# Folding two layer norms into weights, statistics of two tiles at once and one bank for four heads' sums, in a two-layer graph-attention, Mamba and LSTM kernel

## The chip, the cores and the metric

The kernel runs on one core of a Trainium2 chip. The metric is the time of one launch in microseconds of the device. Times given are medians of several runs; the profile is that of one further execution. The engines are named as the profile names them: PE (TensorE, matrix multiplication; its weight loads are PEld), DVE (VectorE), ACT (ScalarE), POOL (GpSimd) and SP (SyncE, which here only starts DMAs).

## The reference, cut to what matters

There are 32 batches of 512 rows of 256 features, and an integer adjacency of 512 x 512 for each batch. Four residual blocks follow each other, each on the normalised features (`_layernorm`: mean out, divided by the root of variance plus 1e-5):

```python
x = x + L0_gnn(_layernorm(x), adj, ...)   # 4 heads of 64; softmax over neighbours; relu + h; a norm per head; gamma, beta
x = x + L0_ffn(_layernorm(x), ...)        # Mamba-2 block: projection, convolution of 4 taps, decayed products, gate, norm, projection
x = x + L1_gnn(_layernorm(x), adj, ...)   # one head of 256; softmax over neighbours; elu
x = x + L1_ffn(_layernorm(x), ...)        # LSTM over 512 steps, with prefix and suffix sums
```

The first three blocks treat every batch by itself ("the layers" below). The LSTM runs over all 32 batches together, one row after another ("the recurrence"); it needs the layers' result of every batch.

## The kernel before, in words

**The whole.** `tile_adj_ffn_kernel` (L1569) calls `layers_per_batch` (L154), which writes the layers' result to `X3` in DRAM, and then `recurrence` (L1290). Between them stands a branch: if a check on the data failed (`odd`), the layers are done again by a general form (`attention0`, `attention1`). With these inputs that form isn't run.

**Tiles.** A batch's features are a tile of 128 partitions x 4 row tiles (`NT`) x 256 columns. Six generators make up a batch: `plain0` (L587, layer-0 attention), `after0` (L428, the norm per head and the residual), `mamba_in` (L703), `mamba_dt` (L715), `mamba` (L788) and `plain1` (L1042, layer-1 attention).

**The order of the work.** It is written out by hand. A `Recorder` (L89) takes down the operations of one batch as units: each operation off PE is a unit, and a run of PE operations into one PSUM bank is a unit. The table `PLAN` (L1535) gives each unit a due time; batch b's units get `PERIOD * b` more (L1145); all units of all batches are sorted by that (L1147) and issued in that order on each engine's queue, which works in order. So every engine has work of three batches mixed: in the steady state PE turns batch b's features and does its attention sums, does the Mamba part of batch b-1 and the layer-1 attention of batch b-2. Buffers and the eight PSUM banks (`LazyPool`, L70) are given out in the same order. The preparation of the recurrence's weights (`recurrence_weights`, L1180) goes on POOL and its DMA queue, in 49 pieces with due times from 32.6 to 34.6 periods (L1133), so among the last batches' units.

**The parts that the change touches.**
- `layernorm` (L138): four `bn_stats` and four `bn_aggr` on DVE, a variance-to-factor step on POOL (`rstd_of`, L129: one `tensor_scalar`, one power), `off` on DVE, and four ACT operations that write the normalised tile (`xn` in `plain0`, `xm` in `mamba_in`, `xg` in `plain1`). Then `transposed` (L369) turns it on PE, eight transposes into two banks, and ACT copies both out.
- `plain0`: `xT` (the turned `xn`) times `w0` gives `hn` (256 features and 12 score columns), copied out by ACT. After the exponents, DVE makes 16 tiles `w` of 128 x 512 (L582), four for each pair (q, m) of a pair of heads and a pair of column tiles. PE multiplies them into `pav` (64 output partitions for each head, L653) and into `psu` (the sums of the softmax, L661):

```python
h, r = 2 * q + k, 32 * (2 * k + t)
nc.tensor.matmul(
    psu[r : r + 32, :], cols[:, 1, h, j : j + 1].to_broadcast([P, 32]), w[:, t, k, :],
    start=(m == 0), stop=(m == NT // 2 - 1),
)
```

  So the four sums of a unit (two column tiles t, two heads k) go to four different quarters of the 128 output partitions. There is one `psu` bank for each q; each is copied by ACT (`avs`), turned by four transposes (`psut`), and DVE adds the two quarters of a head.
- `after0`: for each half of the tile, DVE adds, takes the mean per head, centres; ACT squares; DVE sums the squares; POOL makes the factor; DVE multiplies; POOL applies gamma and the residual.
- `plain1` and `after1` (L984): `xg` is turned and multiplied by `w1`; scores, exponents, four products `pov`; ACT scales each out (`ov`), POOL takes the minimum with zero (`em`, two operations of 128 x 512), ACT the exponential, DVE adds in two operations of 128 x 1024, and the result goes to `X3`.

An f32 matmul in the source is two PE instructions in the profile, and an f32 transpose is one.

Of the kernel before, what the change touches and what calls it, by code (L numbers as in the profile page):

```python
# [9 lines left out]
F32 = mybir.dt.float32  # L10
# [3 lines left out]
AF = mybir.ActivationFunctionType  # L14
ALU = mybir.AluOpType
# [137 lines left out]

def layers_per_batch(ctx, tc, c, a, X3, odd=None, wr=None):  # L154
# [68 lines left out]
    lane = wp.tile([P, 32], F32, name="lane")  # L223
    nc.vector.tensor_reduce(lane, c.ident.rearrange("p (i k) -> p k i", k=32), AX.X, ALU.add)
# [76 lines left out]
    else:  # L301
# [11 lines left out]
        for k in range(DK):  # L313
            pw = score_weights1(k)
            for to, n, f in ((0, 0, 0.8), (1, 1, -0.8), (2, 1, 1.0)):
                nc.vector.tensor_scalar(w1[:, k, D + to : D + to + 1], pw[:, n : n + 1], f, None, ALU.mult)

# [110 lines left out]
    def after0(b, state):  # L428

        x, o, hn = (state[k] for k in ("x", "o", "hn"))  # L430

        G = NT // 2 * H0
        halves = [slice(n * NT // 2, (n + 1) * NT // 2) for n in range(2)]
        ogs = []
        for n, r in enumerate(halves):
            nc.vector.scalar_tensor_tensor(o[:, r], o[:, r], 0.0, hn[:, r, :D], ALU.max, ALU.add)
            og = o[:, r].rearrange("p i (h e) -> p (i h) e", h=H0)
            mean = small.tile([P, G], F32, tag="mean", name=f"mean{b}_{n}")
            nc.vector.tensor_reduce(mean, og, AX.X, ALU.add)
            nc.vector.scalar_tensor_tensor(  # L440
                og, mean.unsqueeze(2).to_broadcast([P, G, HO]), -1.0 / HO, og, ALU.mult, ALU.add
            )
            ogs.append(og)
            yield
        sq = two.tile([P, NT, D], F32, tag="rowa", name=f"sq{b}")
        for n, r in enumerate(halves):
            nc.scalar.activation(sq[:, r], o[:, r], AF.Square)
            vs = small.tile([P, G], F32, tag="vs", name=f"vs{b}_{n}")
            nc.vector.tensor_reduce(vs, sq[:, r].rearrange("p i (h e) -> p (i h) e", h=H0), AX.X, ALU.add)
            rs = rstd_of(nc, small, c, vs, G, 1e-6, scale=1.0 / HO)  # L450
            nc.vector.tensor_tensor(ogs[n], ogs[n], rs.unsqueeze(2).to_broadcast([P, G, HO]), ALU.mult)
            nc.gpsimd.tensor_tensor(o[:, r], o[:, r], gamma.unsqueeze(1).to_broadcast([P, NT // 2, D]), ALU.mult)
            nc.gpsimd.tensor_tensor(x[:, r], x[:, r], o[:, r], ALU.add)
            yield
# [132 lines left out]
    def plain0(b, state):  # L587
# [8 lines left out]
        xn = two.tile([P, NT, D], F32, tag="rowa", name=f"xn{b}")  # L596
        layernorm(nc, small, c, xn, x, NT)
# [7 lines left out]
        yield  # L605
        xT = transposed(xn, "xT", f"xT{b}", psa)
        yield
        hn = one.tile([P, NT, D + 3 * H0], F32, tag="hn", name=f"hn{b}")
        for it in range(NT):
# [6 lines left out]
            nc.scalar.copy(hn[:, it, :], pp[:, : D + 3 * H0])  # L616
# [24 lines left out]
        sums = sall[:, b, :H0, :]  # L641
        for q in range(2):
            rb = spread(line, 2 * q, 2, f"{b}_{q}")
            pa = bank(f"pav{b}_{q}", psa)
            psu = bank(f"psu{b}_{q}", psa)
            for m in range(NT // 2):
# [10 lines left out]
                for t in range(2):  # L657
                    j = 2 * m + t
                    for k in range(2):
                        h, r = 2 * q + k, 32 * (2 * k + t)  # L660
                        nc.tensor.matmul(  # L661
                            psu[r : r + 32, :], cols[:, 1, h, j : j + 1].to_broadcast([P, 32]), w[:, t, k, :],
                            start=(m == 0), stop=(m == NT // 2 - 1),
                        )
                yield
            nc.scalar.copy(avT[:, q, :], pa)
            avs = two.tile([P, N], F32, tag="avs", bufs=1, name=f"avs{b}_{q}")
            nc.scalar.copy(avs, psu)
            pst = bank(f"psut{b}_{q}", psa)
            for i in range(NT):  # L670
                nc.tensor.transpose(pst[:, i * P : (i + 1) * P], avs[:, i * P : (i + 1) * P], c.ident)
            nc.vector.tensor_reduce(
                sums[:, 2 * q : 2 * q + 2, :],
                pst.rearrange("p (i k t r) -> p k i t r", i=NT, k=2, t=2)[:, :, :, :, 0], AX.X, ALU.add,
            )
            yield
        nc.vector.tensor_scalar(sums, sums, TINY, None, ALU.max)
# [25 lines left out]
    def mamba_in(b, state):  # L703
# [3 lines left out]
        layernorm(nc, small, c, xm, x, NT)  # L707
# [334 lines left out]
    def plain1(b, state):  # L1042

        x, adjT = state["x"], state["adjT"]
        xg = two.tile([P, NT, D], F32, tag="rowa", name=f"xg{b}")
        layernorm(nc, small, c, xg, x, NT)
        yield
        gT = transposed(xg, "xT", f"gT{b}", psa)
        yield
        wb = one.tile([P, NT, D + 1], F32, tag="hb", name=f"wb{b}")  # L1050
        pps = []
        for it in range(NT):
# [6 lines left out]
            nc.vector.tensor_copy(exp1[-1][:, it, :], pp[:, D : D + 3])  # L1059
# [3 lines left out]
        yield  # L1063
        for it in range(NT):
            nc.scalar.activation(wb[:, it, :D], pps[it][:, :D], AF.Copy, scale=cols[:, 1, 0, it : it + 1])
# [7 lines left out]
        v = two.tile([P, NT, D], F32, tag="rowa", name=f"ov{b}")  # L1073
        for it in range(NT):
# [8 lines left out]
            rinv = small.tile([P, 1], F32, tag="rinv1", name=f"rinv1_{b}_{it}")  # L1083
            nc.vector.reciprocal(rinv, sums)
            nc.scalar.activation(v[:, it, :], po[:, :D], AF.Copy, scale=rinv)
            yield
        yield from after1(b, x, v)
# [4 lines left out]
    if odd is None:  # L1092
        first, second = attention0, attention1
        STEPS = {mamba_in: 2, mamba_dt: 4, mamba: 25, after0: 4, first: 40, second: 8}
# [195 lines left out]
def recurrence(ctx, tc, c, a, X3, wr, out):  # L1290
# [245 lines left out]
    20597 0 35607 40650 32723 38571 34106 39730 39719 42522 49516 65141 94900 99741 99103 99067  # L1536
    100351 150138 104650 33299 41504 23661 101407 105289 104391 105410 106002 107466 108253 108405 106965 107971
    106773 107370 108940 111668 111723 112606 112816 113281 114035 114669 116368 116572 115240 61098 62220 95465
    106507 111843 123503 73463 118372 125340 127346 127820 128180 128298 129543 130272 130550 131386 131603 131405
    131637 131643 134967 135471 134528 138394 135989 138827 152511 136294 136633 137827 137029 137053 146560 147251  # L1540
    149455 138638 139934 141008 140407 147466 150878 149492 152286 151960 151986 153816 154238 154424 152813 157240
    157367 161054 165376 165719 161319 162074 165950 173469 180373 183224 175030 175764 178029 178951 183005 185109
    191927 190640 193312 196625 199960 199982 203114 203928 197913 197972 197331 199400 204575 205181 204667 206194
    206643 207386 207758 208322 208515 208599 208862 251501 213317 211809 212124 212008 213030 213570 214990 215312
    216196 217020 218298 218575 218670 219478 220078 220205 220492 222048 222692 222696 222880 223352 223622 224029
    224511 224969 225104 226703 225336 228084 228828 234005 236603 228856 237288 257861 259334 246520 239831 270799
    272731 218148 231463 230092 233713 227439 231438 214083 221469 222635 225691 227899 229011 231018 231069 246057
    256887 246081 256048 282617 251804 253984 257648 218528 231970 232380 237266 238842 239097 237276 242576 246641
    248924 251119 253230 216766 225312 226088 232262 232399 235687 227913 239722 240705 245507 246951 252337 238425
    249887 249750 246294 249203 247281 251894 247953 251981 254197 260686 253343 258102 264985 266809 266922 269026  # L1550
    266471 269157 261075 270793 273399 267554 270245 270803 272881 274277 276867 273113 279346 273455 280926 283101
    281800 282500 249960 258452 266090 258433 267917 257968 267949 263228 259624 268875 272648 272216 284851 285585
    292644 294196 268390 280811 280814 282469 279962 279938 281791 284180 282382 284389 285227 273497 283284 284220
    289134 292788 256753 285591 285805 275446 279221 278218 278209 278399 276825 286716 287237 286683 288183 289091
    295346 297865 290911 294061 295192 295528 297194 309768 297695 301052 299601 300411 304806 306262 308890 309432
    311412 312571 311544 312188 312543 314589 316438 317376 323083 314746 322079 314057 319805 327469 327488 330029
    332590 334303 335468 335528 337464 342615 341500 345713 352910 355616 355950 361013 356131 361074 354475 359605
    361130 362268 362402 362989 363334 363970 364961 366465 366763 367927 373957 373956 370932 376447 374494 367135
    374547 374557 374613 374703 381795 387807 390440 393320 385936 391088 392248 394917 381245 383616 389387 393007
    380288 380823 388220 390423 396431 398648 395810 398642 399666 409034 411932  # L1560
# [95 lines left out]
```

## Time and profile before

| what | us |
|---|---|
| median of three runs (3856.74 to 3864.42) | 3859.15 |
| profiled execution | 3853.91 |
| its span, first to last instruction | 3852.2 |
| layers, from the start to the load of the recurrence's weights | 2541 |
| recurrence and output, from there to the end | 1311 |
| first and last `psu` instruction | 56.5 and 2336.3 |
| PE busy in the whole span | 3417.8 (89%) |
| DVE busy in the whole span | 3256.5 (85%) |
| ACT, POOL busy in the whole span | 2403.0 (62%), 1510.6 (39%) |

The page's chain that ended last begins at 2541 us with the DMA that loads the recurrence's weights, so for the layers it says nothing; they are read from the stretches and the timeline. All recorded units of the layers stand on one line (L102, the Recorder), so groups are told apart by the names of their tiles. A line of a timeline gives the start in us, the length in us, the engine and operation, the tile written `<-` the tiles read, the tile mode or shape, and the number of instructions; the bracket says what the engine waited for.

### The profile page before, as it was taken

To read this page: it belongs to the slowest core of one execution; us is meant where nothing else is said; L and a number is where in the kernel's file an instruction comes from. 1 tells how busy PE (TensorE), PEld (TensorE's weight loads), DVE (VectorE), ACT (ScalarE), POOL (GpSimd) and SP (SyncE) were. 2 spreads that over 40 slices of the span, in tenths; PEclk is the share of its full clock that TensorE was granted. 3 is DMA by queue.
4 is the path that set the end of the run, shared out by engine and by line. 5 is a ranking of instruction groups with operands and counts; after the bars stand their busy time and mean duration, and the time that the engine had idled before them with its cause. 6 is when DMAs were issued, how large, how long until landed. Compare 5 with 4: busy or idle time off the path is not lost. (4 is left out here: it accounts for less than half of the span.)

```text
span 3852.2 us, 117182 instructions
## 1 busy us (share of the span) xinstructions
PE 3417.8 (89%) x47370; PEld 2313.5 (60%) x47370; DVE 3256.5 (85%) x10671; ACT 2403.0 (62%) x6434; POOL 1510.6 (39%) x1581
## 2 busy tenths in 40 slices
PE   5999999999999999999999998668888888888882
PEld 3466566556656656655665664446666666666661
DVE  3888888888888888888888886459999999999997
ACT  2777777777777777777777775435454544444441
POOL 3456556555555655655555566710000000000000
PEclk8999999999999999999999998789999999999996
DMA  3322322222223232232223212221222222222226
GB/s 98 89 91 73 101 85 75 94 86 86 83 93 90 72 102 86 72 95 86 86 83 96 87 61 59 82 66 41 44 46 43 46 43 46 43 46 43 46 40 191
DMA packets 271800, 288.76 MB, mean 75 GB/s; under 512 B 151589, under 2 KB 221953, under 8 KB 269073
## 3 DMA queue, kind: packets, MB, share of 16 engines
q1 hardware_dynamic: 265248, 266.96, 25.0%
q10 hardware_dynamic: 3152, 8.76, 0.7%
q8 instruction: 375, 6.14, 0.7%
q0 software_dynamic: 2848, 5.45, 0.5%
q14 instruction: 177, 1.44, 0.1%
HBM read 227.09 MB, written 37.11 MB: 69 GB/s over the span
## 5 line engine op out<-in xcount | busy, mean ns | idle before, releaser
L1413 PE MATMUL pg<-wall,h 128*32 128x96 f32 x16352 | 559.0, 277 | 176.8 <-DVE h L1495 169.4
L1413 PEld LDWEIGHTS pg<-wall,h 128*32 128x32 f32 x16352 | 374.4, 109 | 350.8 <-DVE h L1495 331.9
L1413 PE MATMUL pg<-wall,xTr 128*32 128x96 f32 (+1 forms) x16384 | 549.0, 274 | 0.0
L1413 PEld LDWEIGHTS pg<-wall,xTr 128*32 128x32 f32 x16384 | 447.2, 110 | 5.2 <-issue 0.3
L132 POOL TENSOR_SCALAR ve<-mv 128x4 f32<-128x4 f32 x32 | 6.3, 195 | 1038.5 <-DVE mv L1337 1038.5
L1472 ACT ACTIVATE z<-pg 128x96 f32<-128x96 f32 x512 | 128.7, 251 | 438.9 <-PE pg L1413 438.9
L102 DVE SCALAR_TENSOR_TENSOR w<-rb,colsa,adjT 128x512 f32<-128x512 f32 x512 | 380.4, 778 | 6.0 <-DMA rb<-linea 6.0
L102 DVE SCALAR_TENSOR_TENSOR acc<-px,convw,acc 128x511 f32<-128x511 f32 (+2 forms) x480 | 335.3, 735 | 7.6 <-ACT acc L102 6.4
L1483 ACT ACTIVATE z<-z 128x32 f32<-128x32 f32 x1024 | 234.7, 229 | 168.5 <-DVE z L1481 100.9
L102 ACT ACTIVATE g<-bc,cs 128x128 f32<-128x128 f32 x1024 | 326.0, 399 | 13.1 <-PE py L102 13.1
L102 PE MATMUL px<-mT,win 128*128 128x512 f32 x640 | 307.2, 603 | 0.0
L102 PE MATMUL po<-wc,xh 128*128 128x256 f32 x1024 | 254.3, 392 | 13.5 <-POOL xh L102 8.4
L102 POOL TENSOR_SCALAR ve<-bnmv 128x4 f32<-128x4 f32 x96 | 18.8, 196 | 626.3 <-DVE bnmv L102 607.7
L102 PE MATMUL pav<-w,hb 128*64 128x512 f32 x1024 | 250.1, 608 | 8.0 <-DVE w L102 8.0
L102 PE MATMUL pov<-wb,wv 128*128 128x257 f32 x1024 | 250.5, 392 | 7.0 <-DVE wv L102 5.8
L1495 DVE STREAM_TRANSPOSE h<-hh 128x32 f32<-128x32 f32 x1024 | 216.4, 211 | 34.8
L102 PE MATMUL pz<-mT,win 128*128 128x512 f32 x512 | 245.4, 602 | 0.0
L102 POOL TENSOR_TENSOR rs<-ve,mhalf 128x4 f32<-128x4 f32 (+1 forms) x192 | 237.8, 1239 | 13.3
L1478 DVE SCALAR_TENSOR_TENSOR ab<-z 128x64 f32<-128x64 f32 x1024 | 226.0, 221 | 15.3 <-ACT z L1472 12.0
L102 PEld LDWEIGHTS po<-wc,xh 128*128 128x128 f32 x1024 | 189.5, 193 | 76.6 <-issue 27.0
L1481 DVE SCALAR_TENSOR_TENSOR z<-ab 128x32 f32<-128x32 f32 x1024 | 196.9, 192 | 35.1
L102 POOL TENSOR_SCALAR msk<-adj 128x1024 bf16<-128x1024 int32 x64 | 218.8, 3434 | 13.0 <-DMA adj<-in_adj_dram 7.9
(258 smaller groups left out, 7987.8 us busy)
## 6 DMA issues: line engine op xcount, KB each, us to landing
bc<-line SPq DMA_DIRECT2D x128, 512.0 KB
adj<-in_adj_dram SPq DMA_DIRECT2D x32, 1024.0 KB
rb<-linea SPq DMA_DIRECT2D x64, 512.0 KB
ce<-line SPq DMA_DIRECT2D x64, 384.0 KB
x<-in_x_dram SPq DMA_DIRECT2D x32, 512.0 KB
X<-x SPq DMA_DIRECT2D x32, 512.0 KB
xt<-X SPq DMA_DIRECT2D x128, 128.0 KB
x<-X SPq DMA_DIRECT2D x128, 128.0 KB
```

The costliest lines, as they stand in the source:

```text
L102: return getattr(getattr(self.nc, engine), op)(*map(real, a), **{n: real(v) for n, v in k.items()})
L132: nc.gpsimd.tensor_scalar(ve, var, scale, eps, ALU.mult, ALU.add)
L1413: nc.tensor.matmul(p[q * GB : (q + 1) * GB, :], lhs[k], w[:, k, q, s:e], start=(start and k == 0), stop=(stop and k == DK - 1),)
L1472: nc.scalar.activation(z[:, H : 4 * H], pgs[0], AF.Tanh)
L1478: nc.vector.scalar_tensor_tensor(ab, z[:, c0 + 2 * H : c0 + 4 * H], 1.0, z[:, c0 : c0 + 2 * H], ALU.add, ALU.mult)
L1481: nc.vector.scalar_tensor_tensor(z2[:, c0 : c0 + H], ab[:, :H], 0.5, ab[:, H:], ALU.mult, ALU.add)
L1483: nc.scalar.activation(z[:, (10 + n) * H : (11 + n) * H], z2[:, 4 * n * H : (4 * n + 1) * H], AF.Tanh, scale=0.5)
L1495: nc.vector.transpose(h[n], half)
```

## The change

- **Raw features are turned.** `plain0` and `plain1` transpose `x` itself. `w0` and `w1` (with their score columns) are centred once at the start: a matmul with ones gives each column's sum, and DVE subtracts 1/256 of it (`centred`). The factor `rs` of each row is applied behind the product: in `plain0` by the ACT operation that copies `hn` out; in `plain1` by the DVE operation that copies the score columns out, and by one factor `rs * cols` in the ACT operation that makes `wb`. `xn`, `xg` and their `off` are gone. `mamba_in` keeps its normalised tile.
- **Statistics of two tiles at once.** `two_stats` gives `bn_stats` two row tiles (or two heads) interleaved element by element, so that its sums of even and odd elements are those of the two tiles; no `bn_aggr` is needed. `after0` uses it in place of the two reductions and ACT's squares.
- **One bank for four heads' sums.** Head h's sums go to the output partitions 32h to 32h+31 of one `psu`, and the two column tiles t of a unit go to the same ones. There is one `avs` copy, four transposes and one DVE operation in place of two, eight and three.
- **ELU.** `plain1` writes relu(v) and relu(-v) from the PSUM bank by two ACT operations for each row tile; one exponential of 128 x 1024 with a factor of -1 follows. POOL's minimum is gone, and each row tile has one more tiny DVE operation (the negated factor).
- **Order.** `PLAN` is made anew: 371 units in place of 395; its latest due time is 440741, it was 411932. `PERIOD` (100234) and the 49 pieces stay. An unused tile `lane` is gone.

```diff
+def two_stats(nc, small, src, n, tag):
+    st = small.tile([P, n // 2, 6], F32, tag=f"st{tag}", name="st")
+    for i in range(n // 2):
+        nc.vector.bn_stats(st[:, i, :], src[:, 2 * i : 2 * i + 2, :].rearrange("p i d -> p d i"))
+    s = st.rearrange("p i (k e) -> p (i k) e", k=2)
+    return s[:, :, 1], s[:, :, 2]
...
+        def centred(w, cols, name):
+            pw = bank(name)
+            for k in range(DK):
+                nc.tensor.matmul(pw[:, :cols], ones, w[:, k, :], start=(k == 0), stop=(k == DK - 1))
+            for k in range(DK):
+                nc.vector.scalar_tensor_tensor(w[:, k, :], pw[:, :cols], -1.0 / D, w[:, k, :], ALU.mult, ALU.add)
@@ after0, for each half r @@
             nc.vector.scalar_tensor_tensor(o[:, r], o[:, r], 0.0, hn[:, r, :D], ALU.max, ALU.add)
+            mean, var = two_stats(nc, small, og, G, "a")
+            nc.vector.tensor_tensor(og, og, mean.unsqueeze(2).to_broadcast([P, G, HO]), ALU.subtract)
+            rs = rstd_of(nc, small, c, var, G, 1e-6, scale=1.0 / HO)
+            nc.vector.tensor_tensor(og, og, rs.unsqueeze(2).to_broadcast([P, G, HO]), ALU.mult)
@@ plain0 @@
-        xn = two.tile([P, NT, D], F32, tag="rowa", name=f"xn{b}")
-        layernorm(nc, small, c, xn, x, NT)
+        xT = transposed(x, "xT", f"xT{b}", psa)
+        _, var = two_stats(nc, small, x, NT, "x")
+        rs = rstd_of(nc, small, c, var, NT, LN_EPS, scale=1.0 / D)
...
-            nc.scalar.copy(hn[:, it, :], pp[:, : D + 3 * H0])
+            nc.scalar.activation(hn[:, it, :], pp[:, : D + 3 * H0], AF.Copy, scale=rs[:, it : it + 1])
...
-                        h, r = 2 * q + k, 32 * (2 * k + t)
+                        h = 2 * q + k
                         nc.tensor.matmul(
-                            psu[r : r + 32, :], cols[:, 1, h, j : j + 1].to_broadcast([P, 32]), w[:, t, k, :],
-                            start=(m == 0), stop=(m == NT // 2 - 1),
+                            psu[32 * h : 32 * (h + 1), :], cols[:, 1, h, j : j + 1].to_broadcast([P, 32]), w[:, t, k, :],
+                            start=(j == 0), stop=(j == NT - 1),
                         )
@@ plain1 @@
-        layernorm(nc, small, c, xg, x, NT)
-        gT = transposed(xg, "xT", f"gT{b}", psa)
+        gT = transposed(x, "xT", f"gT{b}", psa)
+        _, var = two_stats(nc, small, x, NT, "x")
+        rs = rstd_of(nc, small, c, var, NT, LN_EPS, scale=1.0 / D)
...
-            nc.vector.tensor_copy(exp1[-1][:, it, :], pp[:, D : D + 3])
+            nc.vector.tensor_scalar(exp1[-1][:, it, :], pp[:, D : D + 3], rs[:, it : it + 1], None, ALU.mult)
...
+        nc.vector.tensor_tensor(rs, rs, cols[:, 1, 0, :], ALU.mult)
...
+            nc.vector.tensor_scalar(rinv[:, 1:2], rinv[:, 0:1], -1.0, None, ALU.mult)
+            nc.scalar.activation(em[:, it, :], po[:, :D], AF.Relu, scale=rinv[:, 1:2])
+            nc.scalar.activation(v[:, it, :], po[:, :D], AF.Relu, scale=rinv[:, 0:1])
             yield
-        yield from after1(b, x, v)
+        nc.scalar.activation(em, em, AF.Exp, scale=-1.0)
+        nc.vector.tensor_tensor(xf, vf, xf, ALU.add)
+        nc.vector.scalar_tensor_tensor(xf, ef, -1.0, xf, ALU.add, ALU.add)
```

## The prediction, made before the result was known

> **What bounds the kernel now.** I read the page's slices first, then one period of the steady state as a stretch, then PE's timeline in it. The recurrence (from 2541 us) has no line of the change in it, so only the layers can move.
>
> ```profile
> PE   5999999999999999999999998668888888888882
> PEclk8999999999999999999999998789999999999996
> ```
>
> From slice 1 to slice 23 (96 to 2310 us) PE is busy nine tenths or more at the full granted clock. One period there, the stretch from 1155.08 to 1229.15 us (columns: PE, PEld, DVE, ACT, POOL, clock, DMA share, GB/s):
>
> ```profile
> 1155.08:1229.15 74.07, 72.41 (x447) 44.67 (x446) 63.66 (x149) 55.70 (x118) 42.42 (x37) 1.00 0.31 87
> ```
>
> PE works 72.4 of 74.1 us, DVE 63.7, ACT 55.7, POOL 42.4. PE bounds the layers; work taken from the other three counts only where PE waits for it. Busy hides waits, though, because a matmul's recorded length overlaps the next one's start. So I count pitches, from start to start in the timeline: 0.43 us for 512 columns, 0.216 for 256, 0.109 for 128, with two tiles of 64 output columns or four of 32 sharing a pitch. In one batch that makes 62 pitches of 0.43 (px 20, pz 16, pav 16, psu 8, pss 2: 26.6), 96 of about 0.217 (po, pov, pwh, phn: 20.9), 122 of 0.109 (transposes and py: 13.3) and about 4.2 for the small ones: 65.0 us. 22 changes of tile mode at about 0.09 add 2.0. The rest of 74.0, **7.0 us per batch, is waiting in PE's fixed order**. That is all that a lighter DVE, ACT or POOL can give back.
>
> **The one bank (psu): a gain off PE, a price on it.** PE's timeline in that period (tile mode, shape, number of instructions):
>
> ```profile
> 1201.76 1.88 PE L102 MATMUL px<-mT,win 128*128 128x512 f32 x4
> ...
> 1212.61 1.94 PE L102 MATMUL pav<-w,hb 128*64 128x512 f32 x8
> 1214.48 2.69 PE L102 MATMUL psu<-w,colsa 128*32 128x512 f32 x16
> 1217.10 1.94 PE L102 MATMUL pav<-w,hb 128*64 128x512 f32 x8
> ...
> 1221.18 0.60 PE L102 MATMUL psut<-ident,avs 128*128 128x128 f32 x4
> 1221.62 0.60 PE L102 MATMUL pgT<-ident,xg 128*128 128x128 f32 x4
> ...
> 1226.14 1.92 PE L102 MATMUL psu<-w,colsa 128*32 128x512 f32 x16
> ```
>
> Look at pav: eight instructions, two at a time (one for each head's 64 output columns), take 1214.48 - 1212.61 = 1.87 us, four pitches of 0.43 and a change of mode. The second psu run does sixteen in 1.85 us (its successor starts at 1227.99): four pitches, four at a time, because the two heads and the two column tiles lie in four different quarters. After the change the two column tiles of a head share a quarter, so only two run at a time: 8 x 0.43 + 0.13 = 3.57 us for sixteen. Before, the two runs took 2.62 and 1.85 us (the first waited for DVE's w tiles). Sum: 2 x 3.57 - 4.47 = **+2.67 us per batch**. The first run's wait of 0.8 is used up in this. Bounds: could the neighbouring units of the other pair of heads run beside it, nothing would be lost; the instruction order of the changed kernel keeps the pairs apart, so I take the full price.
>
> Four of eight psut transposes go: 1221.62 - 1221.18 = **-0.44 us**. One avs copy (0.57, ACT) and some 0.3 of DVE go beside PE's work: nothing.
>
> **Norms folded.** Gone per batch: eight ACT operations of 0.59 us (xn, xg), two `off` (0.27), and ACT's two squares of 0.63. hn's four copies get a factor (0.38 to about the 0.47 of ov). Statistics: six times two bn_stats (412 ns) and two bn_aggr (171 ns) become six of 512 interleaved elements; two pairs of reductions (0.68 each) in after0 become eight bn_stats of 128. Cost of an interleaved one: at best 0.68 us, as a reduction of 512 elements; at worst 4 x 0.36 = 1.44, by the one small read with a stride in the trace (the tile lane: 360 ns for 128 elements, where 128 in line take 283). I take 0.70, since 412 ns for 256 less the 0.15 of a one-element operation, twice, is 0.52 + 0.15. DVE then sheds 10.6 us and takes on 7.1, so -3.5 per batch (+1.5 at the bad end); ACT sheds about 4.5 in all, POOL 3.0 (em).
>
> The Trainium skill, SBUF — State Buffer, "Door 1: The DMA port swizzle", speaks against this: consecutive accesses within a 16-byte line run at full bandwidth, and each crossing to a new line pays, so f32 may stride freely only within four elements. The interleaved read jumps 1 KB at every element. The lane row leans that way (77 ns more), without a reason shown. By the rule DVE would come out no lighter than before, the waits would stay and the sum would lean to 3924; by the row of bn_stats it is the sum below.
>
> None of this lies on PE. What PE gets is waits, in the new order of instructions: (a) pxT no longer waits for xn: its eight took 1.09 us, 8 x 0.109 = 0.87, so -0.2; (b) po waits for DVE's last xh, 4.04 us for sixteen against 3.46; now eight transposes stand between py and po where four quick pm stood, so -0.4 of 0.6; (c) pm and pqa waited 0.25 for the maximum; now psc and half of po stand between, -0.25; (d) 19 changes of mode in place of 22, -0.27. Together **-1.1 us**. The waits for small DVE chains stay: pqv and pcv still follow each other (about 0.9), pdc and prv too (0.4), and DVE's work ahead of pov sums to the same 9.6 us in both orders. Raw turning brings pgT forward to right behind x's update; its last part comes about when PE gets there: 0, at worst +0.5.
>
> So the period changes by 2.67 - 0.44 - 1.1 = +1.1; for a lighter DVE and ACT I allow -0.1: **+1.0 us x 31 = +31 us**.
>
> **Fill and drain.** At the start pxT of batch 0 waits until 36.1 us for xn, which began at 34.5: -2. The centring (four f32 matmuls, four DVE operations of about 0.5) lies before the last weights arrive, and pwc waits for those until 27.9: 0. At the end nothing covers batch 31:
>
> ```profile
> 2485.43 1.66 DVE L102 SCALAR_TENSOR_TENSOR x<-po,rs,x 128x256 f32<-128x256 f32 x4 [4.56 <-POOL rs L102]
> ...
> 2496.42 1.05 POOL L102 TENSOR_TENSOR rs<-ve,mhalf 128x4 f32<-128x4 f32 x1
> 2497.50 0.16 DVE L102 SCALAR_TENSOR_TENSOR off<-bnmv,rs 128x4 f32<-128x4 f32 x1 [8.82 <-POOL rs L102]
> 2497.76 2.08 ACT L102 ACTIVATE xg<-x,off,rs 128x256 f32<-128x256 f32 x4 [18.81 <-DVE off L102]
> 2498.41 2.80 PE L102 MATMUL pgT<-ident,xg 128*128 128x128 f32 x8 [16.02 <-ACT xg L102]
> ...
> 2503.17 0.16 DVE L102 COPY sc<-pwh 128x3 f32<-128x3 f32 x1 [5.51 <-PE pwh L102]
> ```
>
> x is ready at 2487.1, but the row factor stands on POOL behind pieces of the recurrence's weights until 2497.5, and then xg, pgT and pwh follow. Raw, pgT and pwh run meanwhile; only sc waits for the factor, behind ten rows of pieces in place of thirteen, so about 2495 in place of 2503: -8. ELU without POOL saves 1 more. Pieces lie elsewhere among the last three batches' POOL work now, which may cost or give 10.
>
> **Sum.** +31 - 2 - 9 = +20 on the profiled 3853.9 us, 3874. The median lies 5.2 above that execution: **3879 us**. What 0.2% (8 us) doesn't separate counts as the same, about what a measurement of this kernel can tell.
>
> **Rivals.**
> - *PE's waits close (faster).* Mechanism: the new order with a lighter DVE, ACT and POOL covers the chains in front of PE. It decides once the 7.0 us of waits fall below 4.3: price of psu 3.4 in pitches, less 0.44 and 0.27. At 3.5, period -0.8, so -25 - 11: **3823**. For it: DVE and ACT give up about 4 us each, and every wait named ends at one of the two. Against: the two largest chains stand unchanged in the order.
> - *PE pays all and the order adds waits.* 2.67 - 0.44 = +2.2 x 31 = +68, and little from the drain: **3924**. For it: DVE chain raw to da has 5.2 us of cover where it had 6.9, and interleaved statistics may be slow.
> - *It doesn't show.* Waits fall to just what psu costs: **3859**, within 8 us either way.
>
> **Chances.** Forecast 0.47 (0.05 of it within 8 us of no change), closed waits 0.27, all paid 0.15, nothing to see 0.11. So faster 0.27, same 0.16, slower 0.57. Range 3822 to 3930: the second and third cases at its ends.
>
> **What will show it.** psu sixteen instructions in about 3.6 us each time, pairs 0.43 apart; period 75.0 us between the same tiles of neighbouring batches; PE busy at 97% or more; one bn_stats of 128 x 512 near 0.7 us; pgT of the last batch right behind x. Wrong if four psu still run at once, if the period falls below 74.0, or if DVE's stretch grows above 64 us.

## The result and the profile after

Over six runs each the changed kernel takes 3873.47 us (3871.62 to 3876.31) and the kernel before 3858.14 (3856.67 to 3864.42): a ratio of 1.0039, with a 95% interval of 1.0026 to 1.0052. It is slower by 15 us, 0.4%; the forecast was 3879. The profiled execution takes 3873.03 us, its span is 3871.3 (before: 3852.2).

| us | before | after |
|---|---|---|
| first `psu` of batch 0 | 56.5 | 51.7 |
| from there to the first `psu` of batch 31 | 2267.7 | 2312.5 |
| from there to the load of the recurrence's weights | 217.1 | 197.5 |
| load of the recurrence's weights | 2541.3 | 2561.7 |
| period, mean of batches 3 to 28 | 74.00 | 75.42 |

So the layers lose 45 us in the steady state and win back 5 at the start and 20 at the end; the recurrence is the same within 1.3 us. The page's slices:

```profile
PE   5999999999999999999999998758888888888882
PEclk8999999999999999999999999879999999999996
```

From slice 1 to slice 23 PE is still busy nine tenths or more, at the full granted clock. One period, from one batch's praw to the next (columns as before: PE, PEld, DVE, ACT, POOL, clock, DMA share, GB/s):

```profile
1139.90:1215.32 75.42, 72.65 (x453) 45.11 (x447) 64.11 (x137) 52.17 (x109) 38.45 (x35) 1.00 0.29 85
```

ACT gave up 3.5 us and POOL 4.0, but DVE none: 64.1 where it had 63.7. PE's timeline in that period:

```profile
1141.02 5.32 PE L102 MATMUL px<-mT,win 128*128 128x512 f32 x12
1148.06 0.46 PE L102 MATMUL pcs<-tri,da 128*128 128x128 f32 x2 [1.72 <-DVE da L102]
...
1157.58 1.94 PE L102 MATMUL pav<-w,hb 128*64 128x512 f32 x8
1159.44 3.63 PE L102 MATMUL psu<-w,colsa 128*32 128x512 f32 x16
1163.00 3.65 PE L102 MATMUL pav<-w,hb 128*64 128x512 f32 x16
...
1167.86 3.63 PE L102 MATMUL psu<-w,colsa 128*32 128x512 f32 x16
1171.41 1.94 PE L102 MATMUL pav<-w,hb 128*64 128x512 f32 x8
```

Two things are to be seen. Each psu run takes 3.56 us from its start to its successor's (1163.00 - 1159.44), 7.11 for both, where before it was 4.47. And in front of pcs, the product that makes the running sums of Mamba's decay, PE stands idle for 1.72 us until DVE has written da. The waits of PE over ten batches (600 to 1340 us; columns: total in us, times, longest):

```profile
PE pcs L102 <- DVE da L102: 17.2, 10, 1.7
PE pcv L102 <- DVE args L102: 7.8, 10, 0.8
```

The second line stands in the kernel before with the same numbers; the first has no counterpart there. It comes in every batch, 1.7 us each. The statistics, by form, in the same stretch (columns: busy, mean ns, idle before):

```profile
L102 DVE BATCH_NORM_STATS2 st<-x 128x6 f32<-128x512 f32 x59 | 41.1, 697 | 26.8 <-POOL x L102 26.8
L102 DVE TENSOR_TENSOR o<-o,st 128x512 f32<-128x512 f32 x19 | 21.5, 1134 | 0.0
L102 DVE BATCH_NORM_STATS2 st<-o 128x6 f32<-128x128 f32 x76 | 18.3, 283 | 0.0
```

The interleaved bn_stats takes 697 ns, as forecast. The subtraction of the mean (o<-o,st) takes 1134 on average, where the same shape took 677 before: one of its two takes 1.54 us, the other 0.68. The end of the last batch:

```profile
2516.51 1.66 DVE L102 SCALAR_TENSOR_TENSOR x<-po,rs,x 128x256 f32<-128x256 f32 x4 [4.94 <-POOL rs L102]
...
2517.05 0.72 PE L102 MATMUL pgT<-ident,x 128*128 128x128 f32 x2 [2.24 <-DVE x L102]
...
2524.91 1.05 POOL L102 TENSOR_TENSOR rs<-ve,mhalf 128x4 f32<-128x4 f32 x1
2525.99 0.60 DVE L102 TENSOR_SCALAR sc<-pwh,rs 128x3 f32<-128x3 f32 x4 [6.61 <-POOL rs L102]
```

pgT now starts while x is still being written, and only sc waits for POOL's factor. From the end of x to the start of sc it is 7.8 us (2525.99 - 2518.17); before it was 16.1.

### The profile page after: what moved, and what is told of

It reads as the page before. It is cut to its first block, busy times and chain, and to the rows that moved or that the text cites. A ratio compares the mean times of both kernels' runs of the same rounds, so it can differ in the third digit from the quotient of the medians.

```text
span 3871.3 us, 116194 instructions
## 1 busy us (share of the span) xinstructions
PE 3432.4 (89%) x47250; PEld 2318.6 (60%) x47250; DVE 3268.5 (84%) x10258; ACT 2281.8 (59%) x6178; POOL 1381.7 (36%) x1517
## 5 line engine op out<-in xcount | busy, mean ns | idle before, releaser
L102 DVE SCALAR_TENSOR_TENSOR w<-rb,colsa,adjT 128x512 f32<-128x512 f32 x512 | 354.9, 750 | 37.5 <-PE pav L102 19.6
L102 POOL TENSOR_SCALAR ve<-st 128x4 f32<-128x4 f32 (+1 forms) x160 | 34.8, 218 | 737.9 <-DVE st L102 731.4
L102 PE MATMUL px<-mT,win 128*128 128x512 f32 x640 | 290.5, 592 | 0.0
L102 POOL TENSOR_TENSOR rs<-ve,mhalf 128x4 f32<-128x4 f32 (+1 forms) x192 | 251.5, 1310 | 8.2
L102 PE MATMUL po<-wc,xh 128*128 128x256 f32 x1024 | 246.4, 384 | 8.1 <-POOL xh L102 8.1
L102 PE MATMUL psu<-w,colsa 128*32 128x512 f32 x1024 | 232.1, 595 | 0.0
L102 PEld LDWEIGHTS pov<-wb,wv 128*128 128x128 f32 x1024 | 188.0, 193 | 62.2 <-DVE wv L102 12.1
```

Source lines behind the costliest of these rows:

```text
L102: return getattr(getattr(self.nc, engine), op)(*map(real, a), **{n: real(v) for n, v in k.items()})
```

## The experiments

**What was to be told apart.** Theory: PE bounds the layers; the change costs PE 2.2 us of passes (psu and psut), gives back waits in its order, and adds one wait of 1.7 at pcs. Rivals: DVE sets the period, by its sum or by one full stretch; or the waits swallow the price of psu wherever it is paid. Below, each run is set against runs of the kernel before on the same chip (3851 to 3853 us); by the ratio above the changed kernel stands at 3867 there. A period is the mean of batches 3 to 28. Numbers like 254528 are due times of `PLAN`.

### One bank alone

```diff
 kernel before
-            psu = bank(f"psu{b}_{q}", psa)
+        psu = bank(f"psu{b}", psa)
...
-                        h, r = 2 * q + k, 32 * (2 * k + t)
-                            psu[r : r + 32, :], cols[:, 1, h, j : j + 1].to_broadcast([P, 32]), w[:, t, k, :],
-                            start=(m == 0), stop=(m == NT // 2 - 1),
+                        h = 2 * q + k
+                            psu[32 * h : 32 * (h + 1), :], cols[:, 1, h, j : j + 1].to_broadcast([P, 32]), w[:, t, k, :],
+                            start=(j == 0), stop=(j == NT - 1),
```

One avs, psut and maximum remain, as in the changed kernel.

> The kernel before with the one bank for four heads' sums alone; norms, statistics, ELU and due times as before, only the four units that fall away are taken out of the plan. Theory (PE pays each pass of 512 columns that no longer runs beside another): psu 4.47 to 7.11 us per batch as in the changed kernel, psut -0.44, period 74.03 to about 76.2 us, 31 gaps, so +68: about 3926 us. Rival (PE's waits swallow the price, whatever stands around it): the period grows by the 1.4 us of the changed kernel or less, +43 or less: 3901 or below.

Measured: 3906.45 us, ratio 1.0141 (1.0124 to 1.0158), +54 us; period 75.58, +1.6. psu takes 7.11 us and psut 0.49, exactly the price forecast, but 0.6 of the 2.2 comes back in waits elsewhere (0.3 of it at pdc, 0.2 at pxd). The run lies between the two expectations, 5 us above the rival's bound and 20 below the theory's number: the price is paid in full where psu stands, and over a quarter of it is swallowed by waits elsewhere.

### Everything but the one bank

```diff
 changed kernel: psu, avs, psut and the two reductions for each q as in the kernel before
+  168180 169720 170000    due times of avs, psut and the reduction of q = 0; 179869 for the maximum behind that of q = 1
```

> The changed kernel with the two psu banks of before (four column quarters in use at once, eight psut transposes, two avs copies, DVE's two reductions); four units added to its plan, all other due times unchanged. Theory: psu falls from 7.1 to about 4.0 to 4.5 us, psut rises by 0.44, period 75.4 to about 73.2, 31 gaps: -68, about 3805 us, faster than both kernels. Rival (DVE's w tiles, which come at the same pace, set the end of these runs): psu gains no more than a wait in front of pav and psu gives back; period at or above 74.2, no more than -37: 3836 or above.

Measured: 3805.64 us, ratio 0.9878 (0.9862 to 0.9895), period 73.31. That is the theory's number. PE in this kernel:

```profile
1042.41 0.46 PE L102 MATMUL pcs<-tri,da 128*128 128x128 f32 x2 [1.72 <-DVE da L102]
...
1053.80 2.61 PE L102 MATMUL psu<-w,colsa 128*32 128x512 f32 x16
...
1061.83 1.92 PE L102 MATMUL psu<-w,colsa 128*32 128x512 f32 x16
```

The second psu run is back at four quarters at a time. The first still holds a wait of 0.7 us for DVE's w tiles, and pcs waits as long as in the changed kernel. So the norms, the statistics, ELU and the new order together are worth -47 us, the one bank +54 in the old order; the sum, +7, is 8 us short of the measured +15, so the two don't simply add: in the new order the one bank costs 62 (3867 - 3805.6). How much of the -47 is the order's and how much the operations', no run tells.

### pcs later

```diff
 changed kernel, due times
-  pcs 254528, exp 254970, copy 256673
+  pcs 256560, exp 256600, copy 256673
```

> The changed kernel with one PE instruction group moved: pcs, which waits 1.7 us per batch for DVE's da, stands behind px (tile 1) and pz (tile 2) in place of ahead of them (two due times follow it on ACT). Theory (the wait is a gap in PE's fixed order, with DVE ahead of nothing else there): the wait goes, period -1.7, -53 us: about 3820 us. Rival (the chain of DVE itself sets the pace, and the wait turns up at the next product that needs DVE or ACT): period within 0.4 of 75.4, so 3861 or above.

Measured: 3850.46 us, ratio 0.9990 (0.9980 to 0.9999), period 74.69, -0.7. Neither expectation holds. pcs no longer waits, but:

```profile
1065.83 0.38 PE L102 MATMUL pcs<-tri,da 128*128 128x128 f32 x2
...
1072.08 1.94 PE L102 MATMUL pav<-w,hb 128*64 128x512 f32 x8
1074.92 3.63 PE L102 MATMUL psu<-w,colsa 128*32 128x512 f32 x16 [0.91 <-ACT zs L102]
```

pav takes 2.84 us to psu's start where it needs 1.87: more than half of the wait has moved on by nine microseconds. psu multiplies nothing that zs writes, and zs ends 0.05 us before psu starts; what is left to tie them is a PSUM bank, which zs reads empty. And zs is late because ACT's queue, in order, stood behind DVE:

```profile
1068.03 1.28 ACT L102 ACT_TABLE_LOAD   x1 [1.35 <-DVE acc L102]
...
1072.31 1.99 ACT L102 ACTIVATE sqa<-adj,neghalf 128x2048 bf16<-128x2048 int32 x1
...
1074.29 0.57 ACT L102 ACTIVATE zs<-pz 128x512 f32<-128x512 f32 x1
```

acc stands on DVE's queue behind the chain that ends in da. So what makes da late makes acc late too, and through ACT the bank. Moving PE's step doesn't reach that.

### Both

> The changed kernel with both edits: two psu banks of before and pcs behind px and pz. Theory (PE bound, the two gains add): period about 71.5, -121 us: about 3752. Rival (with PE lighter, DVE's chains in front of pav, pcs or po become the bound, so the gains do not add): no more than 20 us below the better of the two single edits.

Measured: 3805.04 us, ratio 0.9876 (0.9860 to 0.9893), period 73.33: the rival. With two banks nothing at all is left of the gain: px falls by 1.78 us, pav rises by 0.97 (zs again) and psu by 0.73 (0.56 of it a wait for w). DVE never idles for more than 0.5 us from raw to the last w there; whatever makes the start of that stretch late makes its end late.

### Two statistics out of that stretch

```diff
 due times                     with both edits above / with two banks, pcs in its old place
-  bn_stats of x 55396, 354502; ve 370338
+  bn_stats of x 78900, 372700; ve 373500
```

> The changed kernel with the two psu banks and pcs behind px and pz (3805 us), and two of the six 512-element bn_stats moved on DVE from between da and the w tiles to behind the last w (POOL's step after one of them follows). Theory (with pcs out of the way, DVE is the bound in the stretch from raw to the last w, where it never idles for more than 0.5 us): the w tiles come 1.4 us sooner, period 73.3 to about 72.0, -40: about 3765 us. Rival (something else in front of pav and psu sets the pace there, such as the buffers of w or the copies out of px): within 10 us of 3805.

> As the kernel with two psu banks (3805.6 us), pcs in its old place, and the same two bn_stats moved behind the last w. Theory (the wait of pcs for da stands ahead of both and stays at 1.7 us; earlier w tiles then find PE still busy): within 10 us of 3805.6. Rival (the w tiles set the pace even with pcs early): -30 to -40, about 3770.

Measured: 3802.82 us, ratio 0.9864 (0.9848 to 0.9881), period 73.06; and 3815.91, ratio 0.9900 (0.9883 to 0.9916), period 73.58. The first misses its theory and falls in the rival's range. pav does fall back to 7.37 us per batch; but psu still waits 0.55 us for w, and the moved statistics make the factor for sc late, so PE waits 0.54 at prv, where it waited less than 0.2. The second ends 10.3 us above 3805.6, just outside the theory's 10, and not for the theory's reason. The w tiles that come sooner do bring something: psu loses its whole wait of 0.7 us (4.40 to 3.71 per batch), although pcs waits 1.7 as before. But the wait at prv costs 0.6, and pxd, pm and pst behind it another 0.4; so a gain and a loss in one edit hide each other.

### Every statistic twice

```diff
 changed kernel, two_stats
         nc.vector.bn_stats(st[:, i, :], src[:, 2 * i : 2 * i + 2, :].rearrange("p i d -> p d i"))
+        if isinstance(nc, Recorder):
+            nc.units[-1][0].append(nc.units[-1][0][-1])
```

> The changed kernel with every bn_stats of the layers' two-tile statistics issued twice in a row (same input, same output): six of 0.70 us and eight of 0.28 us more on DVE, +6.4 us per batch. Theory (PE's fixed order is the bound and DVE counts only in its full stretch from raw to the last w, in which two of the six stand): +0.6 to +1.4 us per batch, +20 to +45: 3890 to 3915 us. Rival 1 (DVE sets the period with its sum): +6.4 x 31 = +200. Rival 2 (DVE is nowhere on the path): within 8 us of the changed kernel.

Measured: 3981.67 us, ratio 1.0337 (1.0320 to 1.0354), period 78.82, +3.4. All three expectations miss. DVE's added 6.4 us are charged to PE at about one half. They aren't charged by the sum (DVE then works 68.9 of 78.7 us), nor only in the full stretch: PE's waits grow at pcs (2.1), at py for g, at po and in front of psu, which are places where a chain through DVE ends at PE. The half is no pure price, though: the recorded lengths of DVE's instructions grow by 6.1 us, and among them the long o<-o,st falls from 1.54 to 0.68 in this order.

### Pieces earlier

```diff
 kernel before
-    todo = [(PERIOD * (nb + 0.6 + 2.0 / 48 * n), nb, n, [lambda: next(pieces, None)], ()) for n in range(PIECES)]
+    todo = [(PERIOD * (nb + 0.3 + 2.0 / 48 * n), nb, n, [lambda: next(pieces, None)], ()) for n in range(PIECES)]
```

> The kernel before with the 49 pieces of the recurrence's weights due 0.3 periods earlier (32.3 to 34.3), nothing else. Theory (the part of the drain that the forecast missed, 153.0 to 143.7 us from the last batch's psu to its pss, comes from where the pieces fall among the last batches' work on POOL): 5 to 15 us less, between 3838 and 3848 on a kernel before at 3853. Rival (the pieces cost the same wherever they stand, and the 9 us came from the lighter ACT and POOL of the change): within 4 us of before.

Measured: 3848.73 us, ratio 0.9990 (0.9980 to 1.0000), 3 us less: the rival's range. From the last batch's psu to its pss it is 149.7 us where it was 153.0. The place of the pieces is good for 3 of the 9 us at most, by this shift; the last run below, which leaves the pieces alone, has 150.7 there. The rest stays open.

### POOL's msk away from the chain

Why is da late? raw is the step width of the Mamba part, turned by PE; a softplus of it, made of small DVE instructions, gives dt, and dt times aneg is da. msk is the adjacency as a mask of zeros and ones. The chain from raw to da takes 4.85 us in the kernel before, in the changed one 6.69. DVE in the changed kernel, and POOL beside it:

```profile
1065.82 0.19 DVE L102 COPY raw<-praw 128x32 f32<-128x32 f32 x1 [0.30 <-PE praw L102]
1066.04 0.19 DVE L102 SCALAR_TENSOR_TENSOR ee<-raw 128x32 f32<-128x32 f32 x1
1066.53 0.64 DVE L102 TENSOR_SCALAR u<-ee 128x32 f32<-128x32 f32 x1 [0.30 <-ACT ee L102]
...
1067.59 0.19 DVE L102 TENSOR_TENSOR u<-u,ee 128x32 f32<-128x32 f32 x1
1067.82 0.19 DVE L102 TENSOR_TENSOR u<-u 128x32 f32<-128x32 f32 x1
1068.05 0.87 DVE L102 TENSOR_SCALAR q<-u 128x32 f32<-128x32 f32 x1
1068.95 2.11 DVE L102 SCALAR_TENSOR_TENSOR q<-q,u 128x32 f32<-128x32 f32 x6
...
1072.31 0.19 DVE L102 TENSOR_TENSOR da<-dt,aneg 128x32 f32<-128x32 f32 x1
```

```profile
1066.10 5.52 POOL L102 TENSOR_SCALAR msk<-adj 128x1024 bf16<-128x1024 int32 x2
```

The same small instructions took 0.18 (u<-ee, q<-u) and 0.19 each (q<-q,u) in the kernel before, where msk ran 5 us after raw, just behind da:

```profile
1054.47 0.18 DVE L102 TENSOR_SCALAR u<-ee 128x32 f32<-128x32 f32 x1
1055.52 0.18 DVE L102 TENSOR_SCALAR q<-u 128x32 f32<-128x32 f32 x1
```

```profile
1058.60 6.98 POOL L102 TENSOR_SCALAR msk<-adj 128x1024 bf16<-128x1024 int32 x2
```

In the changed kernel u<-ee takes 0.64, q<-u 0.87, and one of the six q<-q,u 0.98: 1.9 us more, while msk runs.

```diff
 changed kernel, due times
-  bn_stats of x 79415, ve 79843, msk 62216 and 69577, pow 379657, x + blin 273531
+  bn_stats of x 72150, ve 72400, msk 72500 and 72600, pow 370900, x + blin 270500
```

msk now stands on POOL behind a step that needs a bn_stats right after the last w.

> The changed kernel (one psu bank, pcs in its old place) with POOL's two msk instructions (2.8 us each) put behind the statistics step that now waits for DVE's bn_stats right after the last w; six due times, no operation added or taken. Theory (while msk runs beside the chain raw to da, three DVE instructions in it take 0.64, 0.87 and 0.98 us in place of 0.18 to 0.19, so the chain takes 6.69 us and not 4.85, and that is the 1.7 us that PE waits at pcs): chain 4.85, wait at pcs near 0, period 75.4 to about 73.7, -53: about 3815 us. Rival 1 (those three are slow for another reason, the chain stays at 6.69): within 10 us of 3868. Rival 2 (the chain shortens but what msk takes from the later POOL work, ce, o and xdd, comes back as a wait): -10 to -30.

Measured: 3814.00 us, ratio 0.9900 (0.9884 to 0.9917), period 73.48: the theory's number, and by its mechanism. The chain of this kernel:

```profile
1041.65 0.19 DVE L102 COPY raw<-praw 128x32 f32<-128x32 f32 x1 [0.30 <-PE praw L102]
...
1042.37 0.18 DVE L102 TENSOR_SCALAR u<-ee 128x32 f32<-128x32 f32 x1 [0.29 <-ACT ee L102]
...
1043.42 0.18 DVE L102 TENSOR_SCALAR q<-u 128x32 f32<-128x32 f32 x1
1043.63 1.32 DVE L102 SCALAR_TENSOR_TENSOR q<-q,u 128x32 f32<-128x32 f32 x6
...
1046.20 0.19 DVE L102 TENSOR_TENSOR da<-dt,aneg 128x32 f32<-128x32 f32 x1
```

It takes 4.74 us, and PE's waits no longer name pcs:

```profile
PE pcv L102 <- DVE args L102: 7.8, 10, 0.8
PE pst L102 <- POOL o L102: 2.3, 10, 0.2
```

So the new wait was neither DVE's load nor a shorter cover. PE's cover at pcs is 6.69 - 1.72 = 4.97 us, enough for a chain of 4.74 or 4.85. It was POOL's msk, which the new order of work had put beside the chain. In the period it cost 1.9 us (75.42 - 73.48).

### The same with two banks, and one step more

> The same move of msk with the two psu banks of before (3805 us without the move). Theory: both gains add, since DVE's whole stretch from raw to the last w ends 1.8 us sooner and PE's wait at pcs is gone: period 73.3 to about 71.6, -53: about 3755 us. Rival (as with pcs behind px, the wait only moves to pav and psu): within 10 us of 3805.

Measured: 3787.21 us, ratio 0.9827 (0.9811 to 0.9844), period 72.55, -0.8 against 73.31: between the two. pcs doesn't wait, but a new line stands among PE's waits:

```profile
PE pqv L102 <- DVE mxv L102: 7.2, 10, 0.7
```

mxv is the maximum for layer-1 attention's exponents, which PE spreads (pqv), DVE turns into the arguments (biasv, args) and PE transposes (pcv). DVE makes mxv right behind an addition to o, and this one now runs beside POOL's ce:

```profile
1134.13 1.47 DVE L102 SCALAR_TENSOR_TENSOR o<-o,hn 128x512 f32<-128x512 f32 x1
1135.52 0.28 DVE L102 TENSOR_REDUCE mxv<-prv 128x1 f32<-128x128 f32 x1
```

```diff
 due time of the first o<-o,hn
-  188817
+  189200    behind mxv
```

> The kernel with two psu banks and msk moved (3787 us), and one DVE operation moved: the addition of hn to the first half of o, which takes 1.47 us there beside POOL's product ce (0.69 alone), stands behind mxv in place of ahead of it; one due time. Theory (mxv, and with it pqv, waits for that operation, which is where the 0.7 us per batch at pqv come from): pqv comes 0.7 us sooner, period 72.55 to about 71.8, -22: about 3765 us. Rival (the wait only moves on to pcv or to DVE's statistics of o): within 8 us of 3787.

Measured: 3761.15 us, ratio 0.9764 (0.9748 to 0.9780), period 71.78: the theory's number, and the fastest version of this study, 90 us faster than the kernel before. But the number was hit by luck. The wait at pqv is gone, and pcv, the next product, waits twice as long, as the rival said, mostly because DVE's biasv on the way to args took 0.18 us and now takes 0.80. It ends at 1126.73, as POOL's xdd ends (1126.71):

```profile
PE pcv L102 <- DVE args L102: 15.6, 10, 1.6
```

```profile
1125.93 0.80 DVE L102 TENSOR_TENSOR biasv<-mall,coef 128x3 f32<-128x3 f32 x1
```

Up to pcv only 0.16 us per batch is won; the other 0.6 is won behind it, at pst (0.24), pxd (0.17) and pov (0.16). On DVE one operation there is shorter by 0.86, the first o<-o,st. The changed kernel, and below it this one:

```profile
1107.95 1.00 POOL L102 TENSOR_TENSOR ce<-ce,cT 128x384 f32<-128x384 f32 x1
1107.96 1.54 DVE L102 TENSOR_TENSOR o<-o,st 128x512 f32<-128x512 f32 x1
```

```profile
1129.89 0.68 DVE L102 TENSOR_TENSOR o<-o,st 128x512 f32<-128x512 f32 x1
1129.91 1.52 POOL L102 TENSOR_TENSOR ce<-ce,cT 128x384 f32<-128x384 f32 x1
```

DVE now starts 0.02 us ahead of POOL's ce, and not 0.01 behind it, and it is POOL that takes longer. The kernel that this run starts from has 1.54 there as well. That this gives the 0.6 fits the lines; no run tests it alone.

### msk in the kernel before

```diff
 kernel before, due times
-  msk 33299 and 41504
+  msk 12950 and 13000
```

> The kernel before with POOL's two msk instructions put ahead of the chain raw to da, in place of beside the first w tiles; two due times. Theory (an instruction of DVE with two operands in SBUF stands still beside msk): the w tiles that took up to 1.53 us fall to 0.74, the chain raw to da grows from 4.85 to between 5.3 and 6.5 us where the second msk reaches into it, but PE's cover there is 6.9, so the first psu run loses its wait of 0.8 us: period 74.0 to about 73.2, -25: about 3828 us. Rival 1 (w's tiles aren't what that run waits for): within 8 us of 3853. Rival 2 (the chain takes the loss and PE waits at pcs): slower by 10 to 50.

Measured: 3842.06 us, ratio 0.9976 (0.9967 to 0.9986), period 73.58, -9 us. The w tiles (minimum, median and longest in ns), first in the kernel before, then here:

```profile
L102 DVE SCALAR_TENSOR_TENSOR w<-rb,colsa,adjT x160: 706/737/1529, 616.8 to 1299.9; 128x512 f32<-128x512 f32 x160
```

```profile
L102 DVE SCALAR_TENSOR_TENSOR w<-rb,colsa,adjT x160: 714/742/749, 612.1 to 1291.0; 128x512 f32<-128x512 f32 x160
```

psu falls from 4.47 to 3.71 us per batch, so the wait of 0.8 at its first run was msk beside w. The chain grows to 5.27 us, and PE waits 0.3 at pcs: again a cover of 5.27 - 0.30 = 4.97. The w tiles and the chain do as the theory says. Its cover of 6.9 was wrong, and the wait at pcs makes the gain smaller than forecast, outside all three expectations.

## Why the forecast came out right, point by point

The time was 6 us below the forecast and well inside the range. The closeness is luck: two misses of 13 to 14 us with opposite signs, one in the steady state and one at its ends, cancel, and inside the steady state two more. The profiled execution was forecast at 3874 and took 3873.03; most of the 6 us is the 5.2 that the forecast added for the median, which stands 0.4 above the profiled execution here. The price of psu is the one large term that was right by its mechanism. Of the signs that it named, psu at 3.6 us, bn_stats near 0.70 and pgT right behind x held; the period (75.42 for 75.0), PE's share and DVE's load didn't. The steps, one by one:

- **psu and psut: right.** +2.67 and -0.44 us were forecast, +2.64 and -0.44 measured, also with the one bank alone. Two heads in two quarters run two at a time.
- **Waits given back: too few.** Forecast was -1.1, and 0.1 for a lighter DVE and ACT. Per batch (the order without the msk stall, so that pcs doesn't disturb the count; batches 3 to 28): pxT -0.17 (forecast -0.2), pm and pqa -0.40 (-0.25), po -0.76 (-0.4), and what wasn't named: py -0.45, pov -0.27, pdc -0.27, smaller ones -0.7 (changes of tile mode among them), pst +0.3. Together -2.7.
- **The wait at pcs: missed.** PE idles 1.7 us per batch there, 1.9 of the period. The forecast saw the chain raw to da as the weak place, but only in a rival, and put it down to a cover of 5.2 us in place of 6.9. The cover is 4.97 in both orders; the chain became longer, because msk came to run beside it. The step that failed is "None of this lies on PE": it took each duration on DVE from the old order, and asked of POOL's moved work only who waits for it, not what runs beside it.
- **Period: +1.42, forecast +1.0.** 2.64 - 0.44 - 2.7 + 1.9 = +1.4. Over 31 gaps 45 us in place of 31. The two terms that were off, -1.5 and +1.9, nearly cancel. PE is busy for 96% of it, where 97 or more was to show the forecast right.
- **DVE: not lighter.** -3.5 us per batch was forecast. The recorded lengths of all its instructions fall by 1.5, and its busy time, in which lengths overlap, rises to 64.1, over the mark of 64 that was to show an error. bn_stats came as forecast; what ran beside POOL took back 2.8 (the chain 1.9, the subtraction of the mean 0.9). The forecast's "+1.5 at the bad end" doesn't follow from its own terms: six times 1.44 - 0.70 on top of -3.5 is +0.9.
- **Fill and drain: -24, forecast -11.** From the last pss to the load of the weights 64.0 fell to 53.8 us, -10.2 for a forecast of -9; x to sc alone gave 8.3, where 8 was forecast. The other 9 lie between the last batch's first psu and its pss (153.0 to 143.7), where the forecast had written "may cost or give 10". The pieces' place explains at most 3 of them by the run above; that a lighter POOL and ACT give the rest is argued, not shown. The start gave 5 in place of 2.
- **Rivals.** The waits had to fall below 4.3 us for a gain. 75.4 us less 65.0 + 3.4 - 0.4 of passes and 1.7 of mode changes leaves 5.7. With msk moved the period of 73.5 leaves 3.8, and the kernel is 39 us faster than the one before: the rival with closed waits was the place of two POOL instructions away.
- **The Trainium skill's 16-byte lines** (SBUF — State Buffer, "Door 1: The DMA port swizzle"): bn_stats takes 283, 412 and 697 ns for 128, 256 and 512 elements, 1.0 and 1.1 ns for each further one. The 256 are read in line, while the 128 jump 256 bytes and the 512 jump 1 KB at every element. The rule doesn't show in these DVE reads; the row of bn_stats in the kernel before was the right guide. The lane row was none: it compares a reduction with 32 results with one that has a single result.

## What to carry to other kernels

When an order of work is made anew, look at what each instruction of a short DVE chain runs beside on POOL: its length in the old profile holds only for its old neighbour, and 0.03 us in the starts can decide which of the two is held up. Price a wait at the point where PE meets the chain, as cover less chain, and check both after the change. A price on the bounding engine can be read from pitches to a few hundredths of a microsecond; what the other engines give back can't, and doubling one of their operations tells roughly how much of it reaches the bound (here about one half). When a run hits its number, look where the waits went before you call its reason shown: with o behind mxv the number came and the reason didn't.

## What the runs showed of the hardware

- **DVE and some POOL instructions hold each other up.** Beside msk a TENSOR_SCALAR of 128 x 32 took 0.64 and 0.87 us in place of 0.18, a two-operand one 0.98 in place of 0.19, a w tile up to 1.53 in place of 0.74. Beside POOL's product ce (1.0 us) o<-o,hn took 1.47 in place of 0.69, and half of the o<-o,st 1.54 where the other half, beside POOL's power, took 0.68. Who starts first decides: in the changed kernel the o<-o,st that starts 0.01 to 0.02 us after ce takes 1.54 or 1.55 and ce 1.0 (29 times); in the fastest kernel it starts 0.01 to 0.03 ahead, takes 0.68, and ce 1.5 (28 times). The Trainium skill (SBUF — State Buffer, "SBUF: two separate sides") says that DVE and GpSimd share a pair of ports under an exclusive lock, and that the loser blocks for the whole instruction. The runs agree on the kind, not on the length: in the changed kernel, within the first msk of 2.8 us, u<-u,ee and u<-u took their usual 0.19, and the blocked instructions ended 1.07 and 1.08 us after the start of the two msk, or as the first msk ended. No run shows why.
- **Reading two tiles interleaved cost bn_stats nothing**: 697 ns for 512 elements with a jump of 1 KB at each, against 2 x 412 ns for the same elements in line, and 2 x 171 more for their aggregation.
- **Four or two quarters at once**: sixteen psu instructions take 1.85 us with four column quarters in use, and 3.56 with two.
